# One TensorE stretch for gates r and z, all wide before all narrow matmuls in the later quarters of layer 2, and the last take-up by tiles: a four-layer graph network on one core

## The chip, the cores and the metric

The kernel runs on one core of a Trainium2 chip. The core has a matrix engine (TensorE, PE in the profile, with its weight loads as PEld), a vector engine (VectorE, DVE), a scalar engine for functions and copies (ScalarE, ACT), GpSimd (POOL), and SyncE (SP), which here only issues DMAs. Each engine works through its own queue in order, and they wait for one another by semaphores. Matmul results land in PSUM, which has 8 banks of 128 partitions x 512 fp32. The metric is the device time of one execution in microseconds (us); lower is better.

## The reference, cut to what matters

There are 4096 nodes with 64 features each, and a 0/1 adjacency matrix of 4096 x 4096. Each of four layers normalises x, cuts it at zero, computes something with the adjacency matrix, and adds it to x. Layers 2 and 3 matter here:

```python
# layer 2: two gated steps, then relu
def _ggc(x, adj, W, wih, whh, bih, bhh):
    m = adj @ (x @ W)
    gi = m @ wih.T + bih
    gh = x @ whh.T + bhh
    i_r, i_z, i_n = jnp.split(gi, 3, axis=-1)
    h_r, h_z, h_n = jnp.split(gh, 3, axis=-1)
    r = sigmoid(i_r + h_r);  z = sigmoid(i_z + h_z)
    n = tanh(i_n + r * h_n)
    return (1.0 - z) * n + z * x
h = relu(_ggc(x, adj, W1, ...));  relu(_ggc(h, adj, W2, ...))

# layer 3: hyperbolic midpoint
XW = mobius_matvec(W, X)
num = A @ (gamma * XW);  den = A @ (gamma - 1.0);  alpha = A.sum(1)
# two_mean = num / den, then tanh / artanh of row lengths, relu, exp map
```

Layers 0 and 1 (a decayed neighbour sum, and attention with a sigmoid) come before and aren't touched.

## The kernel before, in words

**Tiling.** Nodes lie in 32 blocks of 128. Four quarters (0 to 3) hold 8 blocks each. The adjacency matrix stays in SBUF as fp8 tiles `A`. A value to be aggregated is split into bfloat16 parts so that the products keep fp32 accuracy: `hm` holds the first two parts side by side (128 columns, a "wide" matmul that fills the 128x128 array), and `lo` the third part (64 columns, a "narrow" matmul, `128*64` in the profile; two of them, on the two halves of the array's columns, run at once).

**Layer 2** (`layer2`, L1488) runs twice, as step 0 and 1. For target quarters 0 and 1 the sums over source quarters 0 to 2 are made as soon as each source is ready; then, quarter by quarter, the rest is summed: for quarters 0 and 1 the last source quarter, for quarters 2 and 3 all four. `sum2` (L1466) makes the 16 wide and 16 pairs of narrow matmuls' worth of one source quarter: wide first, or narrow first if the array is already in the narrow mode and the piece isn't the first. Between wide matmuls it lets `weave.draw` place waiting steps of any engine; between narrow ones no TensorE steps (`draw(False)`). When a quarter is summed, `take2` (L1512) moves it from PSUM to `mx` (ACT copies to `mt`, DVE adds), and a *post chain* begins.

**The post chain of a quarter.** `gates` (L1544): TensorE multiplies `mx` by the gate weights, into four PSUM banks: r and z (profile tile `rz`, `128*64`), and the two halves of n (`ih`, `64*64`). In before, r comes first, then both n parts, and z after the ACT sigmoid of r has been placed. DVE and ACT then make r, tanh, z, and three DVE steps the new `xT`. Step 0 transposes it (`ps_n`) and splits it for step 1. Step 1 transposes it (`ps_o`), adds it to X and runs `pre3` (L1663): layer norm (`mean`, `xc`, `h`), a transpose (`ps_t`), a linear map (`ps_l`), row lengths (`ss`, square roots in DVE steps named `guess`, `nt`, `ny`), an artanh (`axc`, two ACT logarithms `at` and `ln`, a polynomial `po`), a tanh, and at last `S3`, the three-part bfloat16 operand of layer 3. ACT loads another function table between sigmoid or tanh, and the logarithm.

**Layer 3** (`layer3`, L1735) makes eight units u of 512 target nodes. One unit has four result columns of 128 nodes, each the sum of 32 matmuls `acc<-S,A`, 1024 in all. `sum3` (L1715) keeps a unit in two PSUM banks, two columns each; the last unit, 7, has three banks (2, 1, 1 columns: tiles a, b, c). Units 0 to 2 first take source quarters 0 and 1 and are put aside (early take-ups), units 3 to 5 take quarters 0 to 2 as far as their banks go, then quarter 3 for all, and units 6 and 7 at the end. `take3` (L1795) moves a unit from PSUM: per bank two ACT copies (`n`, `alpha`) and two DVE adds. `head3` makes signs and row sums, `post3` the chain of roots, artanh and tanh to the result X and its DMA. `last3` (L1817) does this for unit 7 with a head per tile.

**What sets the order.** The order of each engine's queue is fixed while the program is built. A planner (`Weave`) keeps a clock for each engine with modelled durations; post chains are generators whose next step is placed in a queue when the planner's clock says it can start. `weave.until` and `weave.finish` place steps until a condition holds. So a change of the written order in one place moves steps of other chains. A background chain, `checks`, reads the matrix again in 512 KB tiles `whole` (SP loads, one DVE pass each) to make the flag that decides whether the general kernel has to run; `values_load(flag)` loads it into a register on every engine, before the last unit's take-up.

Of the kernel before, what the change touches and what calls it, by code (L numbers as in the profile page):

```python
# [12 lines left out]
AF = mybir.ActivationFunctionType  # L13
ALU = mybir.AluOpType
# [4 lines left out]
P = 128  # L19
D = 64  # L20
# [550 lines left out]
QB = 8  # L571
CB = 4
# [33 lines left out]
class Weave:  # L606
# [43 lines left out]
    def take(self, kind, make):  # L650

        free = self.banks[kind]
        while not free:
            self.force()
        free.remove(min(free))
        ps = make()
        self.kind[ps.tensor.name] = kind
        return ps

    def free(self, ps):  # L660
        k = ps.tensor.name
        self.banks[self.kind.pop(k)].append(self.used[k][0])
# [134 lines left out]
def fast_kernel(ctx: ExitStack, tc: tile.TileContext, t: dict, out: bass.AP, flag: bass.AP):  # L797
# [10 lines left out]
    nc = tc.nc  # L808
    adjT = t["adjT"]
    N = adjT.shape[0]  # L810
    NB = N // P
# [19 lines left out]
    def b2(name, shape=(P, QB, D), dtype=F32):  # L831
        return b2p.tile(list(shape), dtype, tag="b2", name=name)

    def stat(name, n):
        return small.tile([P, ST], F32, tag="st", name=name)[:, :n]
# [154 lines left out]
    def PE(ins, run, dur, kinds=()):  # L990
        return Op("P", dur, names(*ins), (), run, kinds)
# [474 lines left out]
    def sum2(acc, layer, q, bs):  # L1466

        def wide(stop):
            for b in bs:
                for c in (0, 1):  # L1470
                    add_hm(acc, layer, b, c, a8(q, b)(c), b == 0, stop and b == NB - 1)
                weave.draw()

        def narrow(stop):
            for b in bs:
                for c in (0, 1):
                    add_lo(acc, layer, b, c, a8(q, b)(c), stop and b == NB - 1)
                weave.draw(False)

        if weave.tiled and bs[0]:  # L1480
            narrow(False)
            wide(True)
        else:
            wide(False)
            narrow(True)
        weave.draw()

    def layer2(step, post):  # L1488

        layer = 2 + step  # L1490
        pieces = [range(k * QB, (k + 1) * QB) for k in range(NQ)]
        accs = {}
        for k, bs in enumerate(pieces[:-1]):
            weave.until((layer, k), DONE)
            for q in (0, 1):
                if k == 0:
                    accs[q] = [one(f"acc{c}") for c in (0, 1)]
                sum2(accs[q], layer, q, bs)
        weave.until((layer, NQ - 1), DONE)
        for q in range(NQ):  # L1500
            weave.until(("spill", step, q), DONE)
            load2(step, q)
            if q > 1:
                accs[q] = [one(f"acc{c}") for c in (0, 1)]
            for bs in pieces[-1:] if q < 2 else pieces:
                sum2(accs[q], layer, q, bs)
            if step and q == NQ - 1:
                weave.quiet = True
            take2(q, step, accs.pop(q))
            weave.add(post(q))  # L1510
# [33 lines left out]
    def gates(q, step):  # L1544

        lo, hi = slice(0, D), slice(D, P)
        mx, xT = state.pop((step, q))
        gw, gb = gate_w[step], w(f"gb{step + 1}")
        assert ("gates", step) in DONE
        ps = {}  # L1550

        def gate(name, i):
            for c in (0, 1):
                k = (4 * c + i) * D
                mm(ps[name][lo if c == 0 else hi, :], gw[:, k:k + D], mx[c])

        def reset():
            ps.update(zip(("r", "z", "hn", "in"), several(("rz", "rz", "ih", "ih"))))
            gate("r", 0)

        def news():

            for c, (x, m) in enumerate(((lo, hi), (hi, lo))):
                for own, name, i in ((x, "hn", 2), (m, "in", 3)):
                    k = (4 * c + i) * D
                    mm(ps[name][lo if c == 0 else hi, :], gw[own, k:k + D], mx[c][own, :])

        yield PE(mx, reset, 0.9, [1] * 4)
        yield PE(mx, news, 0.9)
        r = b2("r", (P, CW))  # L1570
        yield AC.activation(r, ps["r"], AF.Sigmoid, bias=gate_b[:, 2 * step:2 * step + 1])
        free(ps["r"])
        yield PE(mx, lambda: gate("z", 1), 0.9)
        yield DV.scalar_tensor_tensor(r, ps["hn"], gb[:, 5:6], r, op0=ALU.add, op1=ALU.mult)
        free(ps["hn"])
        yield DV.tensor_tensor(r, r, ps["in"], ALU.add)
        free(ps["in"])
        z = b2("z", (P, CW))
        yield AC.activation(z, ps["z"], AF.Sigmoid, bias=gate_b[:, 2 * step + 1:2 * step + 2])
        free(ps["z"])  # L1580
        yield AC.activation(r, r, AF.Tanh, bias=gb[:, 2:3])
        yield DV.tensor_tensor(xT, xT, r, ALU.subtract)
        yield DV.tensor_tensor(xT, xT, z, ALU.mult)
        yield DV.tensor_tensor(xT, xT, r, ALU.add)
        return xT
# [126 lines left out]

    dst = {}

    def sum3(u, place, lo, hi):  # L1715

        if u not in dst:

            n = (2, 2) if u < 2 * NQ - 1 else (2, 1, 1)
            v = [x.rearrange("p (k n) -> p k n", n=256)[:, :k] for k, x in zip(n, several(["acc3"] * len(n)))]  # L1720
            dst[u] = lo, v
        start, v = dst[u]
        places = [(x, k) for x in v for k in range(x.shape[1])]
        for d in range(CB):
            ps, k = places[d]
            o = ps[:, k, :W3]
            cols = slice((u % 2) * CW + d * P, (u % 2) * CW + (d + 1) * P)
            for b in range(lo, hi):

                mm(o, A8[u // 2][b // 2][:, b % 2, cols], S3[b // QB, b % QB // CB][:, b % CB, :],  # L1730
                   start=b == start and k == 0, stop=b == hi - 1)
                if b % 4 == 3:
                    weave.draw()

    def layer3():  # L1735

        half = NB // 2
        sets = (0, 1, 2), (3, 4, 5)
        early = {}
        for k in range(2):  # L1740
            for place, u in enumerate(sets[0]):
                weave.until((4, k), DONE)
                sum3(u, place, k * QB, k * QB + QB)
                if k:
                    early[u] = take3(u)
        for k in range(2):
            for place, u in enumerate(sets[1]):
                sum3(u, place, k * QB, k * QB + QB)
        for place, u in enumerate(sets[1][:2]):
            weave.until((4, 2), DONE)  # L1750
            sum3(u, place, half, half + QB)

        weave.until((4, NQ - 1), DONE)
        weave.quiet = False
        while weave.back and weave.back[0][1].e == "D":
            weave.issue(weave.back[0])
        for place, u in enumerate(sets[1]):
            sum3(u, place, half + QB if place < 2 else half, NB)
            summed(u, take3(u))
        for place, u in enumerate(sets[0]):  # L1760
            sum3(u, place, half, NB)
            summed(u, take3(u, early.pop(u)))
        while weave.back:
            weave.force(True)
        sum3(6, 0, 0, NB)
        summed(6, take3(6), alone=True)
        sum3(7, 1, 0, NB)
        others = nc.values_load(flag)
        last3(7)
        weave.finish()  # L1770
        return others

    group, heads = [], []

# [17 lines left out]

    out_nm = out

    def take3(u, more=None, each=None):  # L1795

        e = D + 1
        n65 = b2("n65", (P, CB, e))
        alpha = stat("alpha", CB)
        at = 0  # L1800
        for ps in dst.pop(u)[1]:
            k = ps.shape[1]
            o = n65[:, at:at + k, :]
            S_.activation(o, ps[:, :, :e], AF.Copy)
            S_.activation(alpha[:, at:at + k], ps[:, :, 3 * e], AF.Copy)
            V.tensor_tensor(o, o, ps[:, :, e:2 * e], ALU.add)
            V.tensor_tensor(o, o, ps[:, :, 2 * e:3 * e], ALU.add)
            if each:
                each(n65, slice(at, at + k))
            at += k  # L1810
            free(ps)
        if more is not None:
            V.tensor_tensor(n65, n65, more[0], ALU.add)
            V.tensor_tensor(alpha, alpha, more[1], ALU.add)
        return n65, alpha

    def last3(u):  # L1817

        own = stat("sgn", CB), stat("den", CB), stat("ss", 2 * CB)

        def each(n65, h):
            weave.add(head3(h, n65[:, h], *own))
            piece = weave.work[-1]
            while piece in weave.work:
                weave.issue(piece)

        weave.add(post3([(u, take3(u, each=each))], *own, False))

    def head3(h, n65, sgn, den, ss):

# [145 lines left out]
```

## Time and profile before

| | |
|---|---|
| median of 3 runs | 797.22 us (796.87 to 797.67) |
| profiled execution | 796.95 us |
| its span, first to last instruction | 795.1 us |
| mean granted TensorE clock | 0.993 |
| PE busy | 764.3 us (96%) |
| DVE busy | 637.7 us (80%) |
| ACT busy | 429.9 us (54%) |

The span is 1.85 us shorter than the execution's time. Rows of the profile give the line, the engine, the operation, output tile <- input tiles (buffer numbers left out), shapes and count; nearly all instructions come from two helper lines (L785 for the recorded DVE and ACT operations, L984 for matmuls), so they are told apart by their tiles. Matmuls are pipelined: a row's length is modelled at its end, and its start is what is compared. In brackets stands the engine's idle time before the row, and what ended it.

### The profile page before, as it was taken

How to read it: one execution, taken by the hardware profiler on the slowest of the kernel's cores; microseconds unless marked ns; L12 is line 12 of the kernel's file. 1: busy time of each engine (PE TensorE's matmuls, PEld its weight loads, DVE VectorE, ACT ScalarE, POOL GpSimd, SP SyncE). 2: the span in 40 equal slices, each digit the busy share in tenths (PEclk: the TensorE clock that was granted, in tenths of full speed). 3: DMA queues.
4: the chain of work that ended last, by engine and by line, in shares of the span. 5: the costliest groups of instructions: out<-in, count | busy, mean ns of one | idle time of the engine just before them, and what ended most of it. 6: DMA issues, size and time to landing. Idle time of an engine off the chain costs nothing. (4 is left out here: it accounts for less than half of the span.)

```text
span 795.1 us, 12327 instructions
## 1 busy us (share of the span) xinstructions
PE 764.3 (96%) x4473; PEld 370.4 (47%) x4494; DVE 637.7 (80%) x1436; ACT 429.9 (54%) x760; POOL 63.0 (8%) x129
## 2 busy tenths in 40 slices
PE   6899999999999999999999999999999999999992
PEld 2344444444543333333333334444444444599992
DVE  5876868777878888898998997878779678675896
ACT  5655555555567678778778784122220245444333
POOL 4333232232000000000000000000000000000000
PEclk9999999999999999999999999999999999999997
DMA  9999999999711022012112017696879600000000
GB/s 199 156 195 171 222 164 198 216 164 217 197 40 39 1 85 81 21 45 90 53 37 96 27 31 256 224 336 219 273 251 349 210 9 20 2 1 2 15 28 17
DMA packets 44100, 98.54 MB, mean 124 GB/s; under 512 B 5120, under 2 KB 20608, under 8 KB 44032
## 3 DMA queue, kind: packets, MB, share of 16 engines
q1 hardware_dynamic: 25888, 78.98, 29.3%
q0 software_dynamic: 15984, 14.56, 19.5%
q10 hardware_dynamic: 2160, 4.14, 1.4%
q8 instruction: 37, 0.61, 0.3%
q14 instruction: 31, 0.25, 0.1%
HBM read 136.06 MB, written 5.24 MB: 178 GB/s over the span
## 5 line engine op out<-in xcount | busy, mean ns | idle before, releaser
L785 ACT ACTIVATE sig<-score,fatt_add,fatt_mul 128x512 f32<-128x512 f32 x256 | 177.0, 783 | 47.9 <-PE score L984 41.0
L785 DVE TENSOR_TENSOR sig<-sig,A 128x1024 f32<-128x1024 f32 x128 | 155.0, 1223 | 23.5 <-ACT sig L785 17.8
L785 DVE SCALAR_TENSOR_TENSOR whole<-whole 128x1024 f32<-128x1024 f32 x128 | 153.5, 1219 | 8.2 <-DMA whole<-in_adjT 7.4
L785 ACT ACTIVATE w<-cnt 128x512 int16<-128x512 f32 x198 | 111.7, 595 | 89.3 <-PE cnt L984 86.3
L984 PE MATMUL score<-qd,kT 64*128 64x512 f32 x512 | 124.3, 609 | 0.0
L984 PE MATMUL acc<-sig,S 128*64 128x512 f32 x512 | 118.9, 600 | 1.3 <-DVE sig L785 1.0
L984 PEld LDWEIGHTS <-hm 128*128 128x128 bf16 x768 | 73.5, 98 | 90.9 <-issue 8.6
L984 PE MATMUL acc<-A,hm 128*128 128x512 fp8e4 x512 | 115.3, 379 | 0.0
L984 PE MATMUL cnt<-A,ftri 128*128 128x512 fp8e4 x256 | 98.0, 385 | 6.8 <-ACT A L785 6.0
L984 PE MATMUL cnt<-A,fupd 128*128 128x512 fp8e4 x248 | 95.4, 385 | 5.3 <-DVE w L785 2.1
L984 PE MATMUL acc<-S,A 128*128 128x196 bf16 x1024 | 88.4, 246 | 1.1 <-DVE r L785 1.1
L984 PEld LDWEIGHTS <-A 128*128 128x128 fp8e4 x1024 | 87.1, 97 | 3.2 <-issue 2.9
L984 PEld LDWEIGHTS score<-qd,kT 64*128 64x128 f32 x512 | 50.8, 186 | 68.2 <-issue 55.2
L785 DVE TENSOR_SCALAR w<-cnt 128x512 int16<-128x512 f32 x58 | 40.1, 691 | 39.8 <-PE cnt L984 38.3
L984 PE MATMUL acc<-w,hm 128*128 128x512 bf16 x235 | 70.4, 379 | 0.9 <-issue 0.2
L868 POOL DMA_DIRECT2D A<-in_adjT x111 | 60.9, 550 | 128.3 <-DMA A<-in_adjT 127.0
L984 PEld LDWEIGHTS acc<-sig,S 128*64 128x64 f32 x512 | 33.1, 136 | 78.8 <-issue 58.5
L984 PEld LDWEIGHTS <-lo 128*64 128x64 bf16 x768 | 39.8, 109 | 49.7 <-issue 20.1
L785 ACT ACTIVATE mt<-acc 64x512 f32<-64x512 f32 x32 | 18.9, 591 | 74.6 <-PE acc L984 74.1
L984 PE MATMUL acc<-A,lo 128*64 128x512 fp8e4 x512 | 58.8, 380 | 0.0
L984 PEld LDWEIGHTS <-ftri 128*128 128x128 bf16 x256 | 24.8, 98 | 45.6 <-issue 21.3
L1700 POOL MEMSET S<- 128x4 bf16 x8 | 0.9, 115 | 526.3 <-PE ps_l L984 453.1
(187 smaller groups left out, 637.4 us busy)
## 6 DMA issues: line engine op xcount, KB each, us to landing
whole<-in_adjT SPq DMA_DIRECT2D x128, 512.0 KB, 6.9
A<-in_adjT POOLq DMA_DIRECT2D x111, 128.0 KB, 13.9
qd<-qs SPq DMA_DIRECT2D x16, 128.0 KB, 4.9
mx<-gs SPq DMA_DIRECT2D x16, 128.0 KB, 8.2
xT<-gs SPq DMA_DIRECT2D x8, 256.0 KB, 7.1
x<-in_x SPq DMA_DIRECT2D x6, 256.0 KB, 6.0
xs<-x SPq DMA_DIRECT2D x4, 256.0 KB, 6.0
qs<-qT ACTq DMA_DIRECT2D x4, 256.0 KB, 4.8
```

Of the source, the lines that this page charges most:

```text
L785: return fn(*args, **kw)
L868: nc.gpsimd.dma_start(A8[q][b // 2][:, b % 2, :], a)
L984: nc.tensor.matmul(o, lhsT, rhs, start=start, stop=stop, skip_group_check=True)
L1700: nc.gpsimd.memset(S3[q, c][:, :, 3 * e:], 1.0)
```

## The change

Three places of the code change.

1. `gates`: the z matmuls stand directly behind the r matmuls in one TensorE step (`reset`), with a planned length of 1.8 instead of 0.9, and no longer in a step of their own after r's sigmoid.
2. `layer2`: a late quarter (2 or 3) is given to `sum2` as one range of all 32 blocks, so that its 64 wide matmuls come first and then its narrow ones, in place of four pieces that alternate. Quarters 0 and 1 keep their pieces.
3. `sum3` and `last3`: the last unit is summed with a callback, which is called when a bank is complete: the take-up and head of tile a are placed then, before the matmuls of tile b are, and so on. In before they were placed after all of unit 7's matmuls. The flag's register load moves to just before the last tile's take-up. `take3`'s inner steps become the function `take`. The unused argument `place` is dropped.

```diff
@@ layer2
-            for bs in pieces[-1:] if q < 2 else pieces:
-                sum2(accs[q], layer, q, bs)
+            sum2(accs[q], layer, q, pieces[-1] if q < 2 else range(NB))
@@ gates
         def reset():
             ps.update(zip(("r", "z", "hn", "in"), several(("rz", "rz", "ih", "ih"))))
             gate("r", 0)
+            gate("z", 1)
...
-        yield PE(mx, reset, 0.9, [1] * 4)
+        yield PE(mx, reset, 1.8, [1] * 4)
         yield PE(mx, news, 0.9)
         r = b2("r", (P, CW))
         yield AC.activation(r, ps["r"], AF.Sigmoid, bias=gate_b[:, 2 * step:2 * step + 1])
         free(ps["r"])
-        yield PE(mx, lambda: gate("z", 1), 0.9)
@@ sum3
-    def sum3(u, place, lo, hi):
+    def sum3(u, lo, hi, then=None):
...
                 if b % 4 == 3:
                     weave.draw()
+            if then and k == ps.shape[1] - 1:
+                then(ps, slice(d - k, d + 1))
@@ layer3
-        sum3(6, 0, 0, NB)
+        sum3(6, 0, NB)
         summed(6, take3(6), alone=True)
-        sum3(7, 1, 0, NB)
-        others = nc.values_load(flag)
-        last3(7)
-        weave.finish()
-        return others
+        return last3(7)
@@ take3, last3
+    def take(ps, o, alpha):
+        e = D + 1
+        S_.activation(o, ps[:, :, :e], AF.Copy)
+        S_.activation(alpha, ps[:, :, 3 * e], AF.Copy)
+        V.tensor_tensor(o, o, ps[:, :, e:2 * e], ALU.add)
+        V.tensor_tensor(o, o, ps[:, :, 2 * e:3 * e], ALU.add)
...
-        def each(n65, h):
+        n65, alpha = b2("n65", (P, CB, D + 1)), stat("alpha", CB)
+        others = []
+
+        def then(ps, h):
+            if h.stop == CB:
+                others.append(nc.values_load(flag))
+            take(ps, n65[:, h, :], alpha[:, h])
+            free(ps)
             weave.add(head3(h, n65[:, h], *own))
             piece = weave.work[-1]
             while piece in weave.work:
                 weave.issue(piece)
 
-        weave.add(post3([(u, take3(u, each=each))], *own, False))
+        sum3(u, 0, NB, then)
+        weave.add(post3([(u, (n65, alpha))], *own, False))
+        weave.finish()
+        return others[0]
```

More of the change, by code (lines that the diff above doesn't have):

```diff
@@ L1740, in layer3 @@
         for k in range(2):
-            for place, u in enumerate(sets[0]):
+            for u in sets[0]:
                 weave.until((4, k), DONE)
-                sum3(u, place, k * QB, k * QB + QB)
+                sum3(u, k * QB, k * QB + QB)
                 if k:
@@ L1746, in layer3 @@
         for k in range(2):
-            for place, u in enumerate(sets[1]):
-                sum3(u, place, k * QB, k * QB + QB)
-        for place, u in enumerate(sets[1][:2]):
+            for u in sets[1]:
+                sum3(u, k * QB, k * QB + QB)
+        for u in sets[1][:2]:
             weave.until((4, 2), DONE)
-            sum3(u, place, half, half + QB)
+            sum3(u, half, half + QB)
         weave.until((4, NQ - 1), DONE)
@@ L1756, in layer3 @@
             weave.issue(weave.back[0])
-        for place, u in enumerate(sets[1]):
-            sum3(u, place, half + QB if place < 2 else half, NB)
+        for u in sets[1]:
+            sum3(u, half + QB if u in sets[1][:2] else half, NB)
             summed(u, take3(u))
-        for place, u in enumerate(sets[0]):
-            sum3(u, place, half, NB)
+        for u in sets[0]:
+            sum3(u, half, NB)
             summed(u, take3(u, early.pop(u)))
@@ L1793, in fast_kernel, with take3 @@
     out_nm = out
-    def take3(u, more=None, each=None):
+    def take(ps, o, alpha):
         e = D + 1
-        n65 = b2("n65", (P, CB, e))
-        alpha = stat("alpha", CB)
+        S_.activation(o, ps[:, :, :e], AF.Copy)
+        S_.activation(alpha, ps[:, :, 3 * e], AF.Copy)
+        V.tensor_tensor(o, o, ps[:, :, e:2 * e], ALU.add)
+        V.tensor_tensor(o, o, ps[:, :, 2 * e:3 * e], ALU.add)
+    def take3(u, more=None):
+        n65, alpha = b2("n65", (P, CB, D + 1)), stat("alpha", CB)
         at = 0
         for ps in dst.pop(u)[1]:
[L1802 to L1810, printed above, removed]
+            h = slice(at, at + ps.shape[1])
+            take(ps, n65[:, h, :], alpha[:, h])
             free(ps)
+            at = h.stop
         if more is not None:
@@ L1819, in last3 @@
         own = stat("sgn", CB), stat("den", CB), stat("ss", 2 * CB)
-        def each(n65, h):
+        n65, alpha = b2("n65", (P, CB, D + 1)), stat("alpha", CB)
+        others = []
+        def then(ps, h):
+            if h.stop == CB:
+                others.append(nc.values_load(flag))
+            take(ps, n65[:, h, :], alpha[:, h])
+            free(ps)
             weave.add(head3(h, n65[:, h], *own))
```

## The prediction

> **What bounds the kernel now.** First the page's head and busy table, then the table of stretches cut where the diff acts.
>
> ```profile
> span 795.1 us, 12327 instructions
> PE 764.3 (96%) x4473; PEld 370.4 (47%) x4494; DVE 637.7 (80%) x1436; ACT 429.9 (54%) x760; POOL 63.0 (8%) x129
> ```
> ```profile
> 561.60:685.20 123.60, 123.55 (x754) 55.04 (x754) 99.35 (x236) 37.24 (x68) 0.46 (x4) 1.00 0.49 166
> 685.20:731.10 45.90, 44.79 (x493) 41.72 (x492) 29.66 (x112) 22.84 (x50) 0.46 (x4) 1.00 0.01 2
> 731.10:780.30 49.20, 49.14 (x579) 48.91 (x576) 39.96 (x181) 18.52 (x60) 0.00 (x0) 1.00 0.06 21
> 780.30:795.10 14.80, 0.00 (x0) 0.00 (x0) 7.98 (x49) 4.49 (x14) 0.00 (x0) 0.61 0.04 13
> ```
>
> Columns: stretch, length, busy PE, PEld, DVE, ACT, POOL, clock, DMA. From layer 2's first gates (561.6, where the two programs' orders first part) to the last aggregation matmul, TensorE is busy throughout but for 1.1 us in the second row; the last row is the tail after it. So PE's own time counts one to one up to 780.3, then the DVE/ACT chain. Now PE's rows in order of time; a row's start to the next row's start is what it costs.
>
> ```profile
> 589.72 1.92 PE L984 MATMUL acc<-A,lo 128*64 128x512 fp8e4 x16
> 591.57 2.76 PE L984 MATMUL acc<-A,hm 128*128 128x512 fp8e4 x12
> 595.56 3.64 PE L984 MATMUL acc<-A,lo 128*64 128x512 fp8e4 x32
> 599.14 7.08 PE L984 MATMUL acc<-A,hm 128*128 128x512 fp8e4 x32
> ...
> 627.32 1.08 PE L984 MATMUL rz<-mx,g 128*64 128x512 f32 x4
> 628.33 1.09 PE L984 MATMUL ih<-mx,g 64*64 64x512 f32 x8
> 629.35 1.08 PE L984 MATMUL rz<-mx,g 128*64 128x512 f32 x4
> 630.26 1.90 PE L984 MATMUL acc<-A,lo 128*64 128x512 fp8e4 x16
> ```
>
> 16 narrow take 1.85 (591.57-589.72), 32 take 3.58 (599.14-595.56): one change of array mode is 2x1.85-3.58 = 0.12. The z matmuls (629.35) take 0.91 where narrow follows, the r matmuls 1.01 before ih: 0.10. I take 0.10 per change.
>
> The same view in layer 3:
>
> ```profile
> 693.36 3.57 PE L984 MATMUL acc<-S,A 128*128 128x196 bf16 x40
> 698.05 11.04 PE L984 MATMUL acc<-S,A 128*128 128x196 bf16 x128 [1.11 <-DVE r L785]
> 708.93 0.60 PE L988 MATMUL ps_o<-fident,xT 128*128 128x128 f32 x4
> 717.96 1.08 PE L984 MATMUL ps_l<-W,h3T 128*128 128x128 f32 x8
> ```
> ```profile
> 729.11 0.83 DVE L785 TENSOR_TENSOR S<-s3v,S 128x260 bf16<-128x260 f32 x2
> ```
>
> PE's only stall is 1.11 at 698.05: unit 2 wants PSUM banks that the gates of quarter 3 still hold, because their DVE step r stands behind quarter 2's chain. The last row writes S3 of quarter 3, its two halves ending 729.54 and 729.94; the 449th of the 1024 acc<-S,A matmuls, which first reads it, starts at 731.12, so 1.6 to spare. Last, the tail:
>
> ```profile
> 777.72 0.42 DVE L785 SCALAR_TENSOR_TENSOR n<-n,at 128x256 f32<-128x256 f32 x1
> 782.00 0.21 ACT L785 ACTIVATE n<-acc 128x65 f32<-128x65 f32 x1
> 782.43 0.47 DVE L785 TENSOR_TENSOR n<-n,acc 128x65 f32<-128x65 f32 x2
> 783.98 0.17 DVE L785 RECIPROCAL rc<-den 128x4 f32<-128x4 f32 x1
> 786.88 1.28 ACT L785 ACT_TABLE_LOAD   x1
> 789.62 0.33 SPq L785 DMA_DIRECT2D out_x<-X  x1
> ```
>
> PE ends at 780.24, but DVE, working off unit 6's result (777.72) and then tiles a and b, takes the last tile at 782.43; the shared chain runs from 783.98 to 789.6.
>
> [...]
>
> **The change, part by part.** I read the built order of both programs' engine queues and lay the durations above along it. Up to the first gates the orders are the same.
>
> *Layer 2, PE.* Matmuls are the same in number and shape. Mode changes, counted in the orders, go from 47 to 38 in layer 2 (quarters 2 and 3 of each step change once instead of four times; gates lose one each, some won back where a transpose lands between rz and ih): 9x0.10 = -0.9. Does a moved transpose or gate now wait? From each one's new distance in matmuls (0.216 wide, 0.108 narrow) against its chain: gates of quarter 1 in step 2 come 4.4 after the quarter's end, mx is ready at 3.8; its ps_o comes 18.0 after, xT ready 17.65; quarter 2's ps_o 15.2 after its end, xT 14.6. Slack is 0.35 to 1.6 everywhere, so 0 taken, bound 0 to +1. Narrow stretches (now 6.9 unbroken) issue no PE step of a post chain; the chains' next steps lie in the following wide stretch, which still leaves S3 of quarter 1 ready before quarter 3 ends. SP's order: four instead of two `whole` loads ahead of quarter 1's mx loads; those are needed over 10 us later, loads land in 6.9 (median of the issue table): 0. One check (1.22, with its sums 1.6) and the flag's matmul move from layer 2 to after S3; PE's flag matmul follows the first use of S3 by 28x0.085 = 2.4 and its input by 2.0: no wait. DVE's first take-up there starts 1.1 later; DVE has 1.98 idle at 742.57 in the trace, so it catches up: 0.
>
> *Layer 3, start.* T is layer 2's end (685.20 before). In the new order 40 S matmuls (3.4), then r with z (1.92), ih (1.02), quarter 2's ps_t (0.44), 16 S, its ps_l (0.92). DVE's r steps now stand ahead of quarter 2's length sums and run at T+6.6 to 8.0; z's sigmoid ends T+8.3; unit 2 wants banks at T+9.8. The 1.11 stall is gone. But the rest of quarter 3's gates (three xT steps, 0.69 each) stands in DVE behind quarter 2's chain and all six early take-ups. Along the queue: sums from T+10.55 (ACT frees at mxn), 4.23 to `at` (as 693.11 to 697.34), first xT T+16.7, then 12 adds (about 0.32 each), gam to at 1.05, s3v 0.9, four S steps 0.43 each, last xT at T+24.8. PE reaches ps_o, now after 248 S matmuls instead of 208, at T+25.5: 0.7 to spare. From there the chain's own length decides: ps_t follows by 76 S, ps_l by 16 more, at T+34.2; S3 is ready 729.54-717.96 = 11.58 after ps_l's start, T+45.8. PE arrives after 0.92 plus only 108 S (9.18; 144 before), T+44.3. It waits about 1.5. First use at T+45.8 against 731.12-685.20 = 45.92: -0.1 net, with the two mode changes saved here inside. The stall moves from the banks to S3.
>
> *Tail.* In the new DVE order unit 6's chain stops in the middle of its square root, and tile a (PE done 774.7) is taken at 775.2; then the root's end, tile b at 777.9 to 779.5, then axc at 779.47. On ACT the last tile's copy now stands behind unit 6's two Ln (779.7 to 780.15), the Tanh table load (to 781.45) and its first Tanh: it starts at 781.7, or 782.0 if the flag's load costs its 0.3 gap (777.49 to 777.80) there too. DVE then takes the tile at 782.0 to 782.4, no earlier than 0.4 before now. And unit 6's last three DVE steps (at, n, X: 777.52 to 778.60, 1.0 with overlap) stand between the last tile's sums and rc. Together +0.6 to +0.9; I take +0.7. The old cover for these three, the wait for PE, is gone.
>
> Sum: -0.9 - 0.1 + 0.7 = -0.3 on the profiled 796.95 (span 795.1 plus 1.85 around it); the median of the runs is 0.27 above it: 797.22 - 0.3 = 796.9.
>
> **Rivals.**
> A. *It does what it says.* S3's chain keeps pace and the tail shortens. Then -0.9, -1.11 and two changes -0.2, and the tail ends when PE plus one take-up allows: copy 0.2 after 780.24, take-up and head 1.6, rc at 782.3 + the 1.0 above = 783.3, -0.6: 794.4. For: PE has room at ps_o. Against: 108 matmuls can't hold 11.58.
> B. *Half of it:* either S3 doesn't wait (-1.5) or the tail gains 0.6 instead of losing 0.7: 795.5. For: a single lag of a few tenths on ACT decides the tail.
> C. *Small waits in layer 2:* the 0.35-0.7 slacks fall short two or three times: 797.7.
> D. *Slower: xT of quarter 3.* Six early take-ups ahead of it on DVE each wait for ACT's copies, which themselves stand behind the table load. It decides from T+25.5 on: each microsecond past that delays ps_o, ps_l and S3 one to one, with nothing left to fill PE. If DVE needs 3 more (each take-up 0.5 longer), 2.4 is added: 799.3. For: in the trace ACT copies and DVE adds of these units are PE-paced with 1.0 gaps. Against: here PE is ahead.
>
> **How the numbers follow.** 0.2% (1.6 us) is about what a measurement of this kernel can tell from no change. Forecast 0.46 at 796.9, own range 796.0 to 797.8; A 0.13, B 0.15 (a little over half of it beyond 0.2%), C 0.11, D 0.15. Faster 0.13+0.08 = 0.21, same 0.46+0.07+0.11 = 0.64, slower 0.15. The range leaves about half of A and of D out: 794.9 to 799.0.
>
> **What would show it.** PE's view in layer 2: one change of mode per late quarter, each 0.2 to 0.4 shorter, no waits; one PE wait of 1.5 on S (from DVE) some 45 us after layer 2's end and none on r; rc 0.7 later after PE's end (4.4 instead of 3.7), with X<-X,n of unit 6 directly before it. Wrong if PE shows waits on xT, mx or h, if S3 is awaited for under 0.5 or over 3, or if rc follows PE's end by less than 3.7.

## The result, and the profile after

The changed kernel takes 795.74 us (median of 20 executions, 795.31 to 796.44) against 797.17 us before in the same session (20 executions, 796.76 to 797.84). The ratio is 0.9981, with a 95% interval of 0.9975 to 0.9988: 1.4 us less, just inside the 0.2% that the prediction called "no change", and 1.2 us under the 796.9 that it named. The profiled execution took 796.44 us.

The page's head and busy table of the changed kernel:

```profile
span 794.7 us, 12336 instructions
PE 764.4 (96%) x4494; PEld 370.7 (47%) x4494; DVE 636.3 (80%) x1436; ACT 428.3 (54%) x759; POOL 62.1 (8%) x129
```

The span is only 0.4 us shorter than before's 795.1, which hides most of the gain. The table of stretches shows why. First one row for the kernel before, cut at its real first gates, then the rows of the changed kernel; the columns are those of the prediction (stretch, length, busy PE, PEld, DVE, ACT, POOL, clock, DMA share, GB/s).

```profile
528.35:685.20 156.85, 156.80 (x954) 69.32 (x954) 125.36 (x278) 47.34 (x84) 0.46 (x4) 1.00 0.56 184
```
```profile
529.43:684.55 155.12, 155.12 (x951) 69.63 (x950) 119.89 (x262) 46.56 (x82) 0.46 (x4) 1.00 0.56 186
684.55:730.30 45.75, 44.45 (x494) 41.80 (x492) 31.82 (x123) 21.91 (x50) 0.47 (x4) 1.00 0.01 2
730.30:779.80 49.50, 49.42 (x578) 48.88 (x578) 41.80 (x186) 17.73 (x60) 0.00 (x0) 1.00 0.05 18
```

Layer 2 begins 1.08 us later in this execution (529.43 against 528.35), although up to there both programs have the same order; over all profiled kernels of this study that moment lies between 528.3 and 529.4. So stages are compared, not spans. Exact starts give:

| stage | before | after | difference |
|---|---|---|---|
| layer 2, first gate matmul to first `acc<-S,A` | 156.85 | 155.12 | -1.73 |
| layer 3 up to the first use of S3 of quarter 3 | 45.93 | 45.76 | -0.17 |
| from there to PE's end | 49.12 | 49.42 | +0.30 |
| PE's end to the last `rc` | 3.73 | 4.14 | +0.41 |
| `rc` to the last instruction | 11.09 | 10.78 | -0.31 |
| sum | 266.72 | 265.22 | -1.50 |

The sum agrees with the medians' -1.43. The gain is layer 2's, and it is larger than forecast.

PE's rows in order of time, layer 2, changed kernel; they answer to the split gates of before:

```profile
588.82 1.88 PE L984 MATMUL rz<-mx,g 128*64 128x512 f32 x8
590.63 1.09 PE L984 MATMUL ih<-mx,g 64*64 64x512 f32 x8
...
627.82 1.94 PE L984 MATMUL rz<-mx,g 128*64 128x512 f32 x8
629.69 1.09 PE L984 MATMUL ih<-mx,g 64*64 64x512 f32 x8
```

r and z together take 1.87 at 627.82 (629.69 - 627.82), where a wide matmul stands before them, as at six of layer 2's seven joined stretches, and 1.81 at 588.82, where a narrow one does. Before, r took 1.01 and z 0.91, 1.92 together. The same view in layer 3, and DVE's row for S3:

```profile
710.04 0.60 PE L988 MATMUL ps_o<-fident,xT 128*128 128x128 f32 x4
...
718.74 1.08 PE L984 MATMUL ps_l<-W,h3T 128*128 128x128 f32 x8
719.65 9.35 PE L984 MATMUL acc<-S,A 128*128 128x196 bf16 x108
730.32 2.61 PE L984 MATMUL acc<-S,A 128*128 128x196 bf16 x28 [1.31 <-DVE S L785]
732.86 0.19 PE L984 MATMUL flag_ps<-fones,odds 128*1 128x1 f32 x2
```
```profile
729.83 0.83 DVE L785 TENSOR_TENSOR S<-s3v,S 128x260 bf16<-128x260 f32 x2
```

The 1.11 stall on the banks is gone, and PE waits 1.31 for S3 instead. The flag's matmul has come from layer 2 to 732.86. The tail, DVE's rows and one of ACT:

```profile
774.71 0.62 DVE L785 TENSOR_TENSOR n<-n,acc 128x130 f32<-128x130 f32 x2 [0.61 <-ACT alpha L785]
...
780.24 0.36 DVE L785 SCALAR_TENSOR_TENSOR po<-po,x 128x4 f32<-128x4 f32 x2 [0.49 <-DVE po L785]
...
783.53 0.43 DVE L785 TENSOR_TENSOR X<-X,n 128x256 f32<-128x256 f32 x1
783.88 0.17 DVE L785 RECIPROCAL rc<-den 128x4 f32<-128x4 f32 x1
```
```profile
781.03 0.21 ACT L785 ACTIVATE n<-acc 128x65 f32<-128x65 f32 x1
```

Tile a is awaited for 0.61 in the middle of unit 6's chain (774.71), the flag's register load leaves 0.49 idle on DVE (780.24; before 0.29), and unit 6's last X stands directly before `rc`.

### The profile page after: what moved, and what is told of

Read it like the earlier page. It is cut to its first block, busy times and chain, and to the rows that moved or that the text cites. A ratio compares the mean times of both kernels' runs of the same rounds, so it can differ in the third digit from the quotient of the medians.

```text
span 794.7 us, 12336 instructions
## 1 busy us (share of the span) xinstructions
PE 764.4 (96%) x4494; PEld 370.7 (47%) x4494; DVE 636.3 (80%) x1436; ACT 428.3 (54%) x759; POOL 62.1 (8%) x129
## 3 DMA queue, kind: packets, MB, share of 16 engines
q10 hardware_dynamic: 2160, 4.14, 1.4%
## 4 chain that ended last, share of the span: by engine, by line
PE 84%; DVE 8%; ACT 3%; DMA 2%; issue 1%; SPq 0%; ACTq 0%; DVEq 0%
PE acc L984 52%; PE score L984 13%; PE cnt L984 12%; PE rz L984 2%; PE ps_l L984 1%; ACT sig L785 1%; PE ps_t L988 1%; DVE ss L785 1%; DVE sig L785 1%; PE ih L984 1%; DMA x<-in_x 1%; DVE nt L785 1%; ACT w L785 1%; PE ps_kq L984 1%; DVE w L785 1%
## 5 line engine op out<-in xcount | busy, mean ns | idle before, releaser
L984 PE MATMUL acc<-w,hm 128*128 128x512 bf16 x256 | 75.5, 379 | 0.3 <-DVE hm L785 0.3
L984 PEld LDWEIGHTS <-fupd 128*128 128x128 bf16 x248 | 24.4, 98 | 38.4 <-issue 14.0
```

Source lines behind the costliest of these rows:

```text
L984: nc.tensor.matmul(o, lhsT, rhs, start=start, stop=stop, skip_group_check=True)
```

## The experiments

Each kernel was timed beside the kernel before, which took 797.1 to 797.2 us in every session; ratios are against it. "Layer 2" and so on are the stages of the table above, from each kernel's profile.

**The parts alone.** Gates: the edit of `gates` on the kernel before.

> Only r and z in one stretch. Theory (prices from the two traces: 0.10 us per change of array mode, 0.05 per joined r-z pair, a wait for S3 where too few matmuls stand ahead of it): layer 2 has 45 changes instead of 49 and 7 joins, -0.75; layer 3's start has the changed kernel's order (108 S matmuls between ps_l and S3), so the wait of 1.1 on DVE r is gone and one of 1.3 to 1.5 on S3 comes, with three changes less: 0 to -0.2. In all -0.8 (796.4 against 797.2). Rival (the gain belongs to the long wide and narrow runs, not to the gates): no difference, 797.1 to 797.3, and no wait on S3.

Measured 795.81 us, ratio 0.9985 (0.9978 to 0.9991): 1.3 us less, where 0.8 was expected. Layer 2 takes 155.76, 1.09 less instead of 0.75; the bank stall is gone, and S3 is awaited for 1.31, as in the changed kernel. So this edit alone swaps the one stall for the other, and it alone brings most of the gain. Its mode changes in layer 2 fall by 4 only (49 to 45; these counts take in the flag's matmul and the change into the first gates, which the prediction's 47 leaves out), worth 0.4.

The trace gives the rest, if each matmul's start is compared with the next one's. r and z are two passes each, a pass being two matmuls that start 0.007 apart. A pass takes 0.43, and 0.53 when the next matmul is of another mode; but a pass that itself stands first behind a change takes 0.05 more, 0.48. Within a stretch of layer 2, in the kernel before and in the changed one, a wide matmul, or a pair of narrow ones, takes 0.216; the last before a change takes 0.31, and the first behind one 0.24 if narrow and 0.226 if wide. So a change of mode is paid on both sides: 0.10 before it, and behind it 0.05 by a gate pass, 0.02 by a narrow stretch, 0.01 by a wide one. In the kernel before, all 14 stretches of r or z in layer 2 begin behind a change; here only 3 of the 7 joined ones do (6 of 7 in the changed kernel). That is 11 times 0.05, 0.6 less; 0.1 to 0.2 goes back, mostly because eight more narrow stretches begin behind a change. And a short wait goes that the view doesn't mark as idle time:

```profile
645.18 1.05 PE L984 MATMUL ps_l<-W,h3T 128*128 128x128 f32 x8
646.28 0.63 PE L988 MATMUL ps_o<-fident,xT 128*128 128x128 f32 x4
```

This is the kernel before: `ps_l`'s eight matmuls take 1.10 to the next row where 0.90 is usual (719.65 - 718.74 above is 0.91), because the transpose behind them comes too early: its `xT` is ready at 646.14 only. With the gates joined this 0.2 is gone. 0.4 + 0.6 - 0.15 + 0.2 makes 1.05 of the 1.09.

Late quarters: the edit of `layer2` on the kernel before.

> Only the late quarters' order, gates as before. Theory: only 47 changes instead of 49, since the three gate stretches now fall inside wide runs and change the mode four times each: -0.2. Only 92 S matmuls stand between ps_l and S3: 11.58 - 0.92 - 92 x 0.085 = 2.8 of wait on S3, against 1.1 on r before: +1.7. In all +1.3 (798.5). Rival (the long runs carry the gain): -0.8 or more (796.4 or less).

Measured 800.13 us, ratio 1.003 (1.0018 to 1.0043): 3.0 us slower, where +1.3 was expected. Layer 2 (-0.22, with -0.2 forecast) and the wait for S3 (2.67, with 2.8) came as forecast. The surplus lies behind the wait. PE's rows and the table of stretches of this kernel:

```profile
721.77 7.99 PE L984 MATMUL acc<-S,A 128*128 128x196 bf16 x92
732.43 7.76 PE L984 MATMUL acc<-S,A 128*128 128x196 bf16 x70 [2.67 <-DVE S L785]
```
```profile
729.00:732.40 3.40, 0.75 (x9) 0.52 (x7) 3.07 (x14) 1.66 (x4) 0.00 (x0) 1.00 0.00 0
732.40:735.90 3.50, 3.47 (x23) 3.16 (x23) 0.70 (x3) 0.34 (x2) 0.00 (x0) 0.53 0.00 0
735.90:739.40 3.50, 3.50 (x43) 3.50 (x41) 2.11 (x9) 0.99 (x5) 0.00 (x0) 0.99 0.00 0
```

For 3.5 us after the wait the granted clock is 0.53, and PE does 23 matmuls where the next 3.5 us hold 43. They start 0.163 us apart instead of 0.083; twenty of them make 1.6 us. Behind the 1.31 us wait of the changed kernel the clock stays 1.00. Two more runs, below, test this.

Tail: the edits of `sum3`, `layer3`, `take3` and `last3` on the kernel before, and the changed kernel without them.

> Only the last take-up by tiles. Theory: layers 2 and 3 as before up to PE's end, the reciprocal of the last chain 0.4 later after PE's end (4.1 instead of 3.7), time 0.1 to 0.5 longer (797.3 to 797.7). Rival (the tail part does what it says): the reciprocal earlier than 3.7 after PE's end and the time 0.3 to 0.6 shorter.

> Gates and late quarters changed, last take-up as before. Theory: TensorE as in the changed kernel (38 changes of mode in layer 2, wait of 1.3 on S3), reciprocal 3.7 after PE's end: 0.1 to 0.5 faster than the changed kernel, so -1.5 to -1.9 against before (795.3 to 795.7). Rival (the tail carries part of the gain): slower than the changed kernel, 796.0 to 796.4.

With the tail edit alone 797.26 us, ratio 1.0004 (0.9996 to 1.0012); without it 795.14 us, ratio 0.9974 (0.9963 to 0.9984), both just under the theory's ranges. In the profiles the edit puts `rc` 0.40 later after PE's end (4.13 and 4.14 with it, 3.73 and 3.76 without), and 0.3 of it comes back behind `rc` (what shortens that part wasn't found). The stages differ by about 0.1 net, which the first run can't tell from nothing; the median of the second is 0.6 better than the changed kernel's, with overlapping intervals and no stage that shows it. On top of the joined gates, the late quarters take another 0.6 off layer 2 (155.76 to 155.17; 0.1 of it is the flag's matmul, which moves to layer 3).

**One mode change by itself.** The late quarters in eight half pieces instead of four whole ones, on the kernel before.

```diff
-            for bs in pieces[-1:] if q < 2 else pieces:
+            for bs in pieces[-1:] if q < 2 else [range(k, k + QB // 2) for k in range(0, NB, QB // 2)]:
```

> The kernel before, with late quarters summed in eight half pieces that alternate wide and narrow, so that layer 2 changes the array's mode 74 instead of 49 times with the same matmuls. Theory (0.10 each): +2.5 (799.7), all of it in layer 2 on PE without a wait. Rival (changes are mostly hidden, and the gain of the changed kernel is in the joined gates or in waits): +0.8 or less.

Measured 800.10 us, ratio 1.0038 (1.0025 to 1.0052). Layer 2 takes 159.56, 2.71 more for 25 more changes: 0.108 each. The hidden 0.2 at 646.28 doesn't occur in this run, so the price may be up to 0.12; the prediction's 0.10 was nearly right, and a cost of 0.8 or less for all of them, as the rival had it, is out.

**The wait for S3 filled.** Unit 5's 32 matmuls of quarter 2 are put ahead of the first use of S3, in the changed kernel, in the one without the tail edit, and in the kernel before.

```diff
-        for u in sets[1][:2]:
+        for u in sets[1]:
             weave.until((4, 2), DONE)
...
-            sum3(u, half + QB if u in sets[1][:2] else half, NB)
+            sum3(u, half + QB, NB)
```

> The changed kernel with unit 5's 32 matmuls over source quarter 2 moved ahead of the first use of quarter 3's S3: 140 instead of 108 S matmuls behind ps_l, 0.92 + 140 x 0.085 = 12.8 against the chain's 11.58. Theory: the wait on S3 (1.31) is gone and comes nowhere else: 1.3 faster than the changed kernel, -2.7 against before (794.4). Rival (PE's lead is lost at the next wait, for banks or take-ups, which DVE makes later than before): the wait is gone but PE's end moves by under 0.5, time within 0.4 of the changed kernel.

> The same, with the last take-up as before the change. Theory: no wait on S3 and the earlier reciprocal: 0.1 to 0.5 below the run with the fill and the tiles, -2.8 to -3.2 against before (794.0 to 794.4). Rival (tiles help once PE ends earlier): slower than it by 0.2 or more.

> The kernel before, with the same 32 matmuls moved ahead. Theory: S3 had 1.6 to spare there, so nothing waits less: PE still waits 1.1 on r, time the same within 0.2. Rival (the earlier matmuls are a gain by themselves): 0.5 or more faster.

Measured 795.66 us (0.9981, 0.9975 to 0.9988), 794.81 us (0.9971, 0.9961 to 0.9981) and 798.58 us (1.0016, 1.0007 to 1.0024). All three theories missed: 794.4, 794.0 to 794.4, and no change were expected. The wait is gone in the first two, and layer 3's matmuls end 1.5 us sooner after layer 2 (so the rival of the first had the time right, but not its reason), but up to the last X the tail takes back 1.3 and 0.8 of it; in the kernel before, which had no wait to fill, the edit costs 0.85 at `rc`, and the rest of the 1.5 in its median wasn't found. The prediction's picture, PE's time one to one up to its end, can't give that. DVE's rows from S3 on show what does; here the kernel before, and then it with the edit:

```profile
733.05 0.61 DVE L785 TENSOR_TENSOR n<-n,acc 128x130 f32<-128x130 f32 x2 [3.11 <-ACT alpha L785]
...
767.61 0.17 DVE L785 TENSOR_TENSOR at<-at,ny 128x12 f32<-128x12 f32 x1 [0.28 <-ACT at L785]
...
777.52 0.16 DVE L785 TENSOR_TENSOR at<-at,ny 128x4 f32<-128x4 f32 x1 [0.32 <-ACT at L785]
...
778.89 0.62 DVE L785 TENSOR_TENSOR n<-n,acc 128x130 f32<-128x130 f32 x2 [0.29 <-DVE X L785]
```
```profile
736.20 0.61 DVE L785 TENSOR_TENSOR n<-n,acc 128x130 f32<-128x130 f32 x2 [5.83 <-ACT alpha L785]
```

The rows at 733.05 and 736.20 are the take-ups of the first unit that is complete. The 32 matmuls stand ahead of it, so DVE starts on it some 3 us later. Before, DVE then waits for PE twice more (1.98 at 742.57 and 0.24 at 749.94), and from 749.94 to `rc` at 783.98 it is idle only 0.28, 0.32 and 0.29 at a time, for ACT's tanh twice and the flag's load, never for PE. With the edit even the 1.98 is gone. Without the tail edit the two kernels give the balance, counted from layer 3's start: the first unit's take-up comes 1.2 later (50.52 against 49.35), the 1.98 falls away, and `rc` comes 0.7 sooner (98.22 against 98.94). The end is DVE's: from that take-up to `rc` it has 47.7 us, of which it is idle 1.5 in five short waits.

**DVE's work in the tail.** If so, `rc` must move with DVE's queue although PE is long done. In the kernel with the fill and without the tail edit, first the flag's register load is put last, then also unit 6's last addition on GpSimd.

```diff
-        others = nc.values_load(flag)
         last3(7)
         weave.finish()
-        return others
+        return nc.values_load(flag)
```

> The kernel with the gate and late-quarter edits, unit 5's matmuls of quarter 2 ahead of S3, and no tail edit (794.81 us), with the flag's register load moved behind the last step of all. There the load stood in DVE's queue before unit 6's last steps, with 0.48 us idle. Theory: the tail is DVE's own time, from unit 6's chain to the last X, so this idle time goes from the end one to one: 794.3 us, rc 0.4 to 0.5 earlier. Rival: the load shows behind the last step instead, or something else sets the end: 794.8 to 795.3 us.

```diff
-            yield DV.tensor_tensor(x, x, v, ALU.add)
+            yield (GP if u == 6 else DV).tensor_tensor(x, x, v, ALU.add)
```

> The same with unit 6's last addition X<-X,n on GpSimd instead of DVE, where it takes 0.43 us. Theory (DVE's own time sets the tail): another 0.35 to 0.43 off, 793.9 us. Rival: [...]ACT's copies set the tail by then: no less than the kernel with the flag's load at the end.

`rc` follows PE's end by 4.59, 4.14 and 3.73: 0.45 less for an idle 0.48, and 0.41 less for a step of 0.43 that now runs on GpSimd (in 0.68, from 776.01). PE's end stands at the same distance from layer 3's start in all three (93.63). So in these kernels DVE's own time sets the tail, one to one. But the times are 795.05 us (0.9973, 0.9964 to 0.9982) and 794.88 us (0.997, 0.9959 to 0.9982), no better than 794.81. For the load the rival was right: with it last, the part behind the last X grows from 5.28 to 5.86, and in no run without this move is it over 5.56. The DMA of the last X lands no later (2.16 behind X instead of 2.42), so what grew comes after it, and the load is paid there. The step on GpSimd keeps its 0.4 up to the last instruction of the profile, but between the two runs' times it doesn't show.

**The clock after a wait.** In the late-quarters kernel the wait is taken away by the same 32 matmuls, and in the changed kernel it is lengthened, by putting unit 4's 32 behind S3.

> The late-quarters edit alone, with unit 5's 32 matmuls of quarter 2 (2.7 us) put ahead of the first use of S3 of quarter 3. In the late-quarters run TensorE waited 2.67 us there, and its next 21 matmuls took 0.163 us each instead of 0.083, 1.65 us more in all. Theory: the long wait itself brings the slow matmuls. Then without the wait both go: TensorE from its first S matmul to its end 98.0 - 2.67 - 1.65 = 93.7 us, all S matmuls near 0.083 us; the tail gives back some 0.8 as in the other two kernels with this edit: 796.6 us. Rival: the slow matmuls have another cause in that place (their operands, or the order of the late quarters): then they stay, TensorE takes 95.3 us, and the time is 798.3 us.

```diff
-        for u in sets[1][:2]:
+        for u in sets[1][:1]:
             weave.until((4, 2), DONE)
...
-            sum3(u, half + QB if u in sets[1][:2] else half, NB)
+            sum3(u, half + QB if u in sets[1][:1] else half, NB)
```

> The changed kernel with unit 4's 32 matmuls of quarter 2 moved from before to behind the first use of S3 of quarter 3, so that TensorE waits there 1.31 + 32 x 0.083 = 4.0 us instead of 1.31. Theory (a long wait brings slow matmuls behind it): some 21 matmuls at 0.163 us follow the wait, TensorE from the first use to its end 49.4 + 2.7 + 1.7 = 53.8 us, and the time is 795.7 + 4.3, less up to 1.0 that DVE catches up in the tail: 799.0 to 800.0 us. Rival (no slow matmuls by the wait): 52.1 us, and 797.4 to 798.4 us.

Filled: 796.75 us (0.9995, 0.9987 to 1.0003), no wait but a hidden 0.1 at the first use of S3, no S matmul of 0.14 us or more behind it, PE from its first S matmul to its end in 93.70 us (93.7 by the theory, 95.3 by the rival). Lengthened: 799.89 us (1.0038, 1.0025 to 1.0052), a wait of 4.03, and behind it

```profile
726.00:729.60 3.60, 0.00 (x0) 0.00 (x0) 3.12 (x14) 1.76 (x6) 0.00 (x0) 0.97 0.01 2
729.60:732.60 3.00, 2.98 (x19) 2.74 (x20) 1.84 (x5) 0.15 (x1) 0.00 (x0) 0.50 0.00 0
```

a clock of 0.50 for 3 us, 18 slow matmuls, and 53.58 from there to PE's end (53.8 and 52.1 were expected). Same matmuls, same operands, slow behind a long wait and not otherwise: the wait brings the half clock. Waits of 2.67 and 4.03 us were enough for it, and those of 1.11 (kernel before) and 1.31 (changed kernel) were not: there the clock stays 1.00.

How long the half clock lasts follows from the late-quarters kernel's rows above: 0.53 over the first 3.5 us and 0.99 over the next come to about 3.4 us of it (an estimate from these two). Where between 1.31 and 2.67 the limit lies, and what sets the moments at which the clock falls and comes back, these runs don't show.

## Why the prediction was right and wrong

"No change" came true, with 1.4 of the 1.6 us allowed, and 795.74 lies in the range of 794.9 to 799.0, but under the likeliest case's own 796.0 to 797.8: the saving was forecast as 0.3. By its steps, with the 0.12 of the flag's matmul taken out of layer 2:

| step | forecast | measured |
|---|---|---|
| layer 2 | -0.9 | -1.6 |
| layer 3 up to S3 | -0.1 | -0.17 |
| flag's matmul moved (0.12 in layer 2, 0.22 in layer 3) | 0 | +0.1 |
| the rest from the first use of S3 to PE's end | 0 | +0.1 |
| tail up to `rc` | +0.7 | +0.41 |
| behind `rc` | 0 | -0.31 |

- **"9x0.10 = -0.9" (layer 2).** The mechanism and the count of nine were right (0.108 by the half pieces), the term was too small, and this is the step that made the forecast miss. It priced only what stands before a change (0.10) and took the matmuls behind it as unchanged. Eight fewer stretches of r and z begin behind a change, at 0.05 each, 0.4, and the transpose at 646.28 had a hidden wait of 0.2, although the text said that PE's only stall was at 698.05. 0.9 + 0.4 + 0.2 = 1.5 of the 1.6. "Slack is 0.35 to 1.6 everywhere, so 0 taken" held: no wait came in.
- **A window.** The text called 561.6 layer 2's first gates; they are at 528.35, and 561.6 is the third quarter's. The counts were made over the whole stage, so the sum isn't touched; but the first row shown there isn't the whole stage.
- **"The stall moves from the banks to S3."** Right in every number: `ps_o` 25.49 us after layer 2's end (25.5), `ps_l` 34.19 (34.2), first use 45.76 (45.8), wait 1.31 (1.5). The rival D, a late `xT`, didn't come.
- **The tail, +0.7.** The order was as told, with unit 6's X directly before `rc`, and the flag's load cost ACT nothing, so the last copy came 1.29 after PE's end and not 1.5 to 1.8. The step that failed is "unit 6's last three DVE steps ... stand between the last tile's sums and rc" with "The old cover for these three, the wait for PE, is gone". There was no such cover: before, too, DVE did these steps in unbroken work. Moving a step within a busy queue cost nothing here; what cost 0.4 were DVE's idle times after 750, 1.38 instead of 0.89 (0.61 for tile a and 0.49 for the flag are new or longer, 0.32 for unit 6's tanh is gone). The 0.61 is the edit's own: it puts tile a's take-up into DVE's queue ahead of unit 6's remaining steps, and there DVE waits for PE. That only 0.1 of the tail's 0.7 was left in the end is luck: the 0.31 behind `rc` wasn't foreseen, and isn't explained.
- **"PE's own time counts one to one up to 780.3."** Wrong as a reading: in the kernel before, from 749.94 on, DVE didn't wait for PE any more. It did no harm here, since the edits saved their time before that.
- **Rivals A and B.** Their times (794.4, 795.5) both lie under the result, and B's is nearer to it than the likeliest case's 796.9. That is luck: their mechanisms, no wait for S3 or a shorter tail, didn't come.

The parts don't add up: -1.3, +3.0 and +0.1 alone, -1.4 together. The late-quarters edit alone makes PE wait 2.67 for S3, behind which the clock is 0.53 for 3.5 us; with the gates joined, S3's chain and the matmuls ahead of it stand otherwise, and the wait is 1.31.

## What to carry to other kernels

Look at the busiest engine's idle times to find where it stops being the bound: the engine that later runs without waiting for it, here DVE from 750 on in the kernel before, sets the end, and then a step moved within its queue is free while every new wait in it is paid (above, `rc` came 0.45 sooner for an idle 0.48). Price a change of mode on both its sides (here 0.10 before it and 0.01 to 0.05 behind it), from the starts of single matmuls, not from the removed changes alone. And keep waits of the matrix engine short: one of 2.67 us cost 1.6 more behind it, and behind one of 1.31 the clock stayed 1.00.

## What the hardware showed unexpectedly

- A wait of 2.67 or 4.03 us of TensorE was followed by a granted clock of 0.53 over 3.5 us and of 0.50 over 3.0; one of 1.11 or 1.31 was followed by 1.00. In the late-quarters kernel two of six executions took 798.1 and 798.7 us, at a mean granted clock of 0.993 and 0.994, and four 800.1 to 800.9, at 0.991 to 0.992; this would fit a half clock that stays away in some of them, but only one of the four has a trace, so it stays open.
- A change of mode was paid on both sides: 0.10 before it, and behind it 0.05 by fp32 gate matmuls (0.48 instead of 0.43 for the first pass), against 0.01 to 0.02 by the fp8 ones. Why they differ isn't known.
- A register load from the flag leaves 0.29 to 0.49 idle on DVE, nothing on ACT behind its table load, and when it is put last it isn't free either: 0.58 behind the last X.
